# Two chained projections of a bidirectional layer, and one merged weight for each direction

## The chip, the cores and the metric

The kernel runs on one core of a Trainium2 chip. A core has a matrix engine (PE, with its weight loads shown apart as PEld), a vector engine (DVE), an activation engine (ACT), a general engine (POOL) and a queue for transfers (SP). Each engine works through its own instructions in the order in which the program issued them, and they wait for each other by semaphores. The metric is the device time of one execution in microseconds (us). The kernel before took 2102.75 us, the median of three runs (2097.81 to 2104.69).

## The reference

Four layers follow each other on a tensor of 2 batches, 1024 positions and 256 channels, all in 32-bit floats: a state-space layer (layer 0), a bidirectional state-space layer (layer 1), and two attention layers (2 and 3). What matters here is layer 1, cut to its projections:

```
mz  = x_ssm @ Wz.T + bz            # 256 -> 512 channels
mx  = x_ssm @ Wx.T + bx            # 256 -> 512
z1  = _ssm(mz @ Wc1.T + bc1, ...)  # 512 -> 512, then the forward scan
z2  = flip(_ssm(flip(mz @ Wc2.T + bc2), ...))   # 512 -> 512, then the backward scan
out = (silu(mx) * z1 + silu(mx) * z2) @ Wf.T + bf + skip
```

`mz` feeds nothing but the two projections `Wc1` and `Wc2`, and no nonlinearity stands between them. So `mz @ Wc1.T` equals `x_ssm @ (Wc1 Wz).T`, with a bias `Wc1 bz + bc1`.

A scan `_ssm` has 512 channels with 16 states each, over 1024 positions. Layer 0 has one scan for each batch, layer 1 two for each batch: six scans in all, s00, s01, s10, s20, s11, s21 (the first digit is 0 for layer 0, 1 and 2 for the two directions of layer 1; the second is the batch).

## The kernel before

**The scans set the order.** `chain` (line 1007) runs the six scans one after the other, each as 64 tiles of 128 rows (32 channels by 4 states) by 1024 positions, taken in pairs. A tile is one decay on ACT (`dA_t`, line 133 with `negA`), one product on POOL (`hb_t`, L952), one scan on DVE (L959 or L963), a second product on DVE (L966) or, for the first tile of some pairs, on POOL (L965), and a sum over states on PE (`fold`, L990), which is issued one pair later. Which engine takes the second product is decided by a running balance (`lead`) of the work that the program counted for DVE and POOL. The decay of the next tile is issued before the current one; there are two buffers of it, so it waits until DVE has finished the tile before the current one.

**Everything else is fitted in between.** The projections and norms of the layers are Python generators in one queue, worked off by `Behind`. Ahead of each tile stands one slot (`Behind.slot`, line 853): it adds a number of credits (`RATES`, line 32: 2048 in the first two scans, then 1250, 1300, 1500, 1500), holds the credit at 2048 at most, and runs steps while credit is above zero. A step costs the columns that its matmuls stream, or the number that it yields, and at least 640. Slots also have an allowance for ACT (2500 for each slot, up to 3400) and POOL (1500, up to 2300). Instructions of a step enter the engines' queues at that place, between those of the scan. Slots are counted here from 1 to 384: 1 to 64 belong to s00, 65 to 128 to s01, and so on.

The queue's order is p00 (layer 0, batch 0), two preparations of conditioning, p01 (layer 0, batch 1), p10 (layer 1, batch 0: norms, `mz`, `mx`, and the inputs of s10), p20 (the inputs of s20), a third preparation, p11 and p21 (the same for batch 1), then layers 2 and 3 of batch 0. p10 can only begin once the output projection of s00 (`residual`, line 802) has run; that is put at the head of the queue five slots after it is registered, which is slot 74. Layer 2 needs the output of s20 and is held until slot 266 and the steps after it. Batch 1 of layers 2 and 3 runs behind the attention that follows the scans.

**The projections.** `projected` (line 506) makes 512 output channels as 4 blocks of 128 by 2 halves of 512 positions. One step issues one block and half: `project` (line 495) calls one matmul for each 128 input channels, so two for a 256-channel source (`mz`, `mx`) and four for a 512-channel source (the two directions). ACT takes the result from one of two PSUM banks (`bank`) and adds the bias; `pipe` (line 375) and `projected` both take a bank back before they fill it a third time. A 32-bit matmul call appears in the profile as two MATMUL instructions.

**The weights.** `weight` (line 348) loads them over the SP queue. Tiles of 128 by 1024 share four buffers; a load whose buffer is still read waits in the SP queue, and what is issued after it waits too. The same queue carries the scan inputs (`sp`, L913), saves (L120) and everything else.

Of the kernel before, what the change touches and what calls it, by code (L numbers as in the profile page):

```python
# [54 lines left out]
def kernel(ctx: ExitStack, tc: tile.TileContext, a: dict, out: bass.AP):  # L55
    nc = tc.nc
# [30 lines left out]
    def dbuf(shape, name):  # L87
        return dram.tile(list(shape), F32, tag=name, name=name)
# [92 lines left out]
    def col(name, i=0, n=1):  # L181
        at, size = _COLS[name]
        assert i + n <= size
        return cols[:, at + i : at + i + n]
# [101 lines left out]
    def cond_first():  # L286

        w = load_k("ada_w0", 2 * D)
        for _ in cond_cols(w, "ada_b0", 4, (2, 0, "ln_g0", "ln_b0", "aff0")):
            pass  # L290

        def gates():
            scb = spread_cond()
            brow, w = abuf((1, D)), abuf((P, 4, D))
            nc.sync.dma_start(brow, a["ada_row0"][:, 2 * D :])
            nc.sync.dma_start(
                w, a["ada_w0"][:, 2 * D :].rearrange("(k p) m -> p k m", p=P)
            )
            yield 3 * T
            cond["gate0"] = []  # L300
            yield from pipe(*(
                cond_rows(
                    [w[:, k, :] for k in range(4)], scb, brow, 0, b, f"gate0_{b}", cond["gate0"]
                )
                for b in range(B)
            ))

        return gates()
# [39 lines left out]
    def weight(name, k, width, at=0, k0=0, slots=0, tag=None):  # L348

        t = wp.tile(  # L350
            [P, k, width], F32, tag=tag or f"w{k * width}", name=f"w_{name}",
            bufs=4 if tag is None and k * width == 1024 else 1,
        )
        src = a[name].rearrange("(k p) m -> p k m", p=P)[:, k0 : k0 + k, at : at + width]
        if slots:
            save(slots, t, src)
        else:
            nc.sync.dma_start(t, src)
        return t
# [373 lines left out]
        )  # L733


    def layer1(b, st1, st2):

        mz = []
        xn = []

        def way(i):
            return [weight(f"c{i}_w", 2, DI, 0, k) for k in (0, 2)]

        def one_way(i, st, wz):
            w_xp, w_dt = weight(f"xp_w{i}", 4, R + 2 * N, slots=2), weight64(f"dt_w{i}", 2)
            st["u"] = dbuf((DI, T), f"u{i}{b}")
            z = []
            yield from projected(
                wz, mz, AF.Identity, lambda m: col(f"bc{i}", m), z, True, st["u"]
            )  # L750
            yield from ssm_inputs(f"{i}{b}", z, w_xp, w_dt, f"dt_b{i}", st)

        def first():
            xt = yield from halves_of(x_of[1][b])
            w_z, w_x = [[weight("xz_w", 2, DI, at)] for at in (DI, 0)]
            st1["x"] = dbuf((T, D), f"x1{b}")
            skip = []
            yield from normed(xt, skip)
            for v in skip:
                nc.vector.tensor_tensor(v, v, twice(cond["s1"][b], 4), ALU.mult)  # L760
                far_op(v, v, twice(cond["o1"][b], 4), ALU.add)
                yield
            o = []
            yield from normed(skip, o)
            for i, v in enumerate(skip):
                far_op(v, v, twice(cond["gate1"][b], 4), ALU.mult)
                yield
                far_op(xt[i], xt[i], v, ALU.add)
                save(3, positions(st1["x"], i), xt[i])
                yield  # L770
            xn.extend(abuf() for _ in range(2))
            yield from channels(
                o, xn, AF.Identity, lambda c: col("n2g", c), lambda c: col("n2b", c)
            )
            yield from projected(
                w_z, xn, AF.Identity, lambda m: col("bz", m), mz
            )
            wz1 = way(1)
            st2["g"] = dbuf((DI, T), f"g1{b}")
            yield from projected(  # L780
                w_x, xn, AF.Silu, lambda m: col("bx", m), [], False, st2["g"], st2["gates"]
            )
            wz2.append(way(2))
            yield from one_way(1, st1, wz1)

        def second():
            yield from one_way(2, st2, wz2[0])

        wz2 = []
        return first(), second()  # L790

    def load_src(src, bias, halves=(0, 1)):
# [740 lines left out]
    with ExitStack() as s:  # L1533
# [13 lines left out]
        p10, p20 = layer1(0, s10.st, s20.st)  # L1547
# [64 lines left out]
        for _ in range(7):  # L1612
            behind.step()
        behind.add(
            cond_first(), cond_later(), p01, p10, p20, cond_last(), p11, p21,
            layer2(0, x2[0], x3[0]), layer3(0, sts[0]),
        )
        chain(
# [23 lines left out]
def _layout(i):  # L1642
# [21 lines left out]
    def heads(v, const_at=None):  # L1664
# [45 lines left out]
        "emb_w2": f["L2_cond_film_emb_W"], "emb_w3": f["L3_cond_emb_w"],  # L1710
        "in_w": f["L0_cond_in_proj_w"].T, "xp_w0": f["L0_cond_x_proj_w"].T,
        "dt_w0": f["L0_cond_dt_proj_w"].T, "out_w0": f["L0_cond_out_proj_w"].T,
        "xz_w": np.concatenate([f["L1_cond_Wx"].T, f["L1_cond_Wz"].T], axis=1),
        "c1_w": f["L1_cond_Wc1"].T, "c2_w": f["L1_cond_Wc2"].T,
        "xp_w1": f["L1_cond_Wdbc1"].T, "dt_w1": f["L1_cond_Wdt1"].T,
        "xp_w2": f["L1_cond_Wdbc2"].T, "dt_w2": f["L1_cond_Wdt2"].T,
# [25 lines left out]
```

## Time and profile before

The profile is one execution. Its own total was not recorded apart from its span, which is 2094.2 us from the first to the last instruction; the median of the runs is 2102.75 us, 8.6 us more, for start and end and for the difference between executions.

| what | us |
|---|---|
| span | 2094.2 |
| scans, from the first scan instruction to the last | 64.5 to 1452.8 |
| attention and what runs behind it, after the last scan | 1459 to 2094 |
| DVE busy, whole span | 1748.3 |
| POOL busy, whole span | 1365.8 |
| PE busy, whole span | 1592.7 |
| ACT busy, whole span | 1140.8 |
| matmuls that read w_xz (mz and mx, both batches), busy | 65.7 |
| matmuls that read w_c1 and w_c2, busy | 129.5 |

How to read it: busy times are shares of an engine's own time, not of the path. Busy time of PE is modelled and overlaps, so that for dense stretches the time from one group's start to the next is the better price. An arrow in a waiting row points to the instruction that ended the wait. "SPq" and the like are an engine's issuing side.

### The profile page before, as it was taken

How to read it: one execution, taken by the hardware profiler on the slowest of the kernel's cores; microseconds unless marked ns; L12 is line 12 of the kernel's file. 1: busy time of each engine (PE TensorE's matmuls, PEld its weight loads, DVE VectorE, ACT ScalarE, POOL GpSimd, SP SyncE). 2: the span in 40 equal slices, each digit the busy share in tenths (PEclk: the TensorE clock that was granted, in tenths of full speed). 3: DMA queues.
4: the chain of work that ended last, by engine and by line, in shares of the span. 5: the costliest groups of instructions: out<-in, count | busy, mean ns of one | idle time of the engine just before them, and what ended most of it. 6: DMA issues, size and time to landing. Idle time of an engine off the chain costs nothing. (4 is left out here: it accounts for less than half of the span.)

```text
span 2094.2 us, 22957 instructions
## 1 busy us (share of the span) xinstructions
PE 1592.7 (76%) x8112; PEld 605.6 (29%) x8112; DVE 1748.3 (83%) x1742; ACT 1140.8 (54%) x1592; POOL 1365.8 (65%) x666
## 2 busy tenths in 40 slices
PE   7576876389685637887955657834999999999997
PEld 3132213033141302222311333201544333333333
DVE  5798898898998999998998999998767657777763
ACT  4665775476546345664555455532154556656665
POOL 0799997998999999899998979997102111000000
PEclk9698988599797558988976978966899999999999
DMA  3673367264853555556763345343200111010001
GB/s 120 253 251 103 130 238 263 69 207 144 289 182 115 188 169 187 179 171 210 251 213 111 103 160 165 122 133 99 82 1 1 39 25 18 24 51 1 1 1 38
DMA packets 112503, 267.55 MB, mean 128 GB/s; under 512 B 16154, under 2 KB 40603, under 8 KB 112388
## 3 DMA queue, kind: packets, MB, share of 16 engines
q1 hardware_dynamic: 112388, 266.09, 38.2%
q8 instruction: 64, 1.05, 0.2%
q14 instruction: 51, 0.42, 0.1%
HBM read 195.91 MB, written 67.90 MB: 126 GB/s over the span
## 5 line engine op out<-in xcount | busy, mean ns | idle before, releaser
L952 POOL TENSOR_TENSOR hb_t<-sp,bc 128x1024 f32<-128x1024 f32 x383 | 918.7, 2436 | 62.9 <-PE ys_t L990 28.7
L133 ACT ACTIVATE dA_t<-sp,negA 128x1024 f32<-128x1024 f32 x384 | 428.3, 1117 | 530.4 <-DVE hb_t L966 446.4
L963 DVE TENSOR_TENSOR_SCAN dA_t<-dA_t,hb_t 128x1024 f32<-128x1024 f32 x195 | 445.8, 2286 | 43.8 <-ACT dA_t L133 29.0
L1442 DVE TENSOR_REDUCE mh<-sc_t 128x1 f32<-128x512 f32 x512 | 327.4, 684 | 114.2 <-PE sc_t L1433 110.6
L990 PE MATMUL ys_t<-hb_t,fold 128*32 128x512 f32 x1536 | 278.7, 735 | 167.2 <-POOL hb_t L965 110.5
L133 ACT ACTIVATE hb_t<-sc_t 128x512 f32<-128x512 f32 x512 | 276.7, 595 | 190.8 <-PE sc_t L1433 190.6
L966 DVE TENSOR_TENSOR hb_t<-dA_t,bc 128x1024 f32<-128x1024 f32 x285 | 349.0, 1224 | 22.1 <-DVE dA_t L959 0.5
L1433 PE MATMUL sc_t<-act_t 32*128 32x512 f32 x2048 | 337.3, 651 | 10.6 <-DVE mh L1442 8.8
L965 POOL TENSOR_TENSOR hb_t<-hb_t,bc 128x1024 f32<-128x1024 f32 x99 | 236.3, 2387 | 16.3 <-DVE hb_t L963 15.6
L799 POOL TENSOR_TENSOR act_t<-act_t,row 128x1024 f32<-128x1024 f32 x8 | 19.1, 2397 | 340.1 <-PE sc_t L99 191.9
L959 DVE TENSOR_TENSOR_SCAN dA_t<-dA_t,hb_t 128x1024 f32<-128x1024 f32 x90 | 205.7, 2285 | 11.8 <-POOL hb_t L952 7.4
L1473 PE MATMUL av_t<-hb_t,act_t 128*32 128x256 f32 x2048 | 164.7, 393 | 1.3 <-DVE act_t L1481 1.3
L95 PE MATMUL bank_t<-act_t,w_c_w 128*128 128x512 f32 x256 | 129.5, 656 | 37.0 <-ACT act_t L133 37.0
L133 ACT ACTIVATE act_t<-bank_t,cols 128x512 f32<-128x512 f32 (+1 forms) x206 | 129.6, 675 | 37.6 <-PE bank_t L95 29.5
L1433 PEld LDWEIGHTS sc_t<-act_t 32*128 32x128 f32 x2048 | 110.7, 186 | 121.4 <-issue 78.3
L990 PEld LDWEIGHTS ys_t<-hb_t,fold 128*32 128x32 f32 x1536 | 39.0, 119 | 362.7 <-POOL hb_t L965 149.5
L963 DVE TENSOR_TENSOR_SCAN hb_t<-dA_t,hb_t 128x1024 f32<-128x1024 f32 x61 | 139.0, 2278 | 4.3 <-ACT dA_t L133 3.9
L141 POOL TENSOR_TENSOR act_t<-act_t 128x1024 f32<-128x1024 f32 x50 | 119.2, 2384 | 0.2
L95 PE MATMUL bank_t<-act_t,w_dt_w 64*128 64x512 f32 x96 | 71.2, 876 | 43.9 <-ACT act_t L133 38.5
L99 PE MATMUL bank_t<-ident,act_t 128*128 128x128 f32 x128 | 34.3, 422 | 91.4 <-ACT act_t L133 91.2
L1473 PEld LDWEIGHTS av_t<-hb_t,act_t 128*32 128x32 f32 x2048 | 42.3, 108 | 191.5 <-issue 178.6
L1378 POOL MEMSET act_t<- 128x1024 f32 x8 | 7.6, 951 | 130.4 <-PE sc_t L1433 130.4
(178 smaller groups left out, 1811.6 us busy)
## 6 DMA issues: line engine op xcount, KB each, us to landing
sp<-dt SPq DMA_DIRECT2D x192, 512.0 KB, 5.5
bc<-bc SPq DMA_DIRECT2D x48, 512.0 KB, 6.8
dt<-act_t SPq DMA_DIRECT2D x48, 512.0 KB, 5.7
u<-act_t SPq DMA_DIRECT2D x24, 512.0 KB, 3.0
fu<-u SPq DMA_DIRECT2D x96, 128.0 KB, 3.4
y<-y SPq DMA_DIRECT2D x96, 128.0 KB, 3.6
g<-act_t SPq DMA_DIRECT2D x16, 512.0 KB, 5.4
fg<-g SPq DMA_DIRECT2D x64, 128.0 KB, 3.2
```

Source lines behind the costliest of these rows:

```text
L95: nc.tensor.matmul(o, w, x, **kw)
L133: nc.scalar.activation(o, x, func, **kw)
L141: nc.gpsimd.tensor_tensor(o, x, y, op)
L952: engine.tensor_tensor(e, self.sp[c, 1], self.bc[0][k], ALU.mult)
L959: nc.vector.tensor_tensor_scan(h[:, ::-1], dA[:, ::-1], e[:, ::-1], 0.0, ALU.mult, ALU.add)
L963: nc.vector.tensor_tensor_scan(h, dA, e, 0.0, ALU.mult, ALU.add)
L965: return lambda: nc.gpsimd.tensor_tensor(e, h, self.bc[1][k], ALU.mult)
L966: nc.vector.tensor_tensor(e, h, self.bc[1][k], ALU.mult)
L990: nc.tensor.matmul(self.ys[d, cp][at : at + DS, :], fold, e[:, ts(ch, 512)], start=False, stop=(k == NK - 1),)
L1433: nc.tensor.matmul(ps, w[r, ts(at, P)], x[r, ts(wide_at, 512)], start=True, stop=True)
L1442: nc.vector.tensor_reduce(mh[n][:, t, ch, j : j + 1], ps, AX.X, ALU.max)
L1473: nc.tensor.matmul(sums.av[32 * j : 32 * j + 32, ts(part, 256)], sts[b]["v"][t // 2][:, t % 2, 4 * g + j, :], es[j // 2][:, at : at + 256] ...
```

## The change

The two chained projections of each direction become one. A new generator `merge` stands in the queue between p01 and p10. For each direction it loads the two halves of the direction's weight, forms `Wc Wz` with matmuls into PSUM (two blocks, four calls of 512 columns each), copies each block with ACT to a tile that stays for the whole program (`way1`, `way2`), forms `Wc bz` with sixteen calls of one column each, and adds the bias with one DVE instruction. p10, p20, p11 and p21 then project from the 256-channel `xn` with these tiles, so each step of a direction issues two calls instead of four, and the eight steps of `mz` with their ACT instructions are gone in p10 and p11. The weights are loaded once instead of once for each batch; `Wz` is loaded untransposed, `Wx` alone. The two resident tiles take 8 KB of each partition; the area set aside for descriptors of software transfers goes from its default to 1024 bytes, and every transfer in the profile is issued by the SP queue.

```diff
+    ways = {}
+
+    def merge():
+
+        w_z = weight("z_w", 4, D)
+        for i in (1, 2):
+            w_c = [weight(f"c{i}_w", 2, DI, 0, k) for k in (0, 2)]
+            w = const.tile([P, 2, DI], F32, tag=f"way{i}", name=f"way{i}")
+            o = const.tile([P, 4], F32, tag=f"wayb{i}", name=f"wayb{i}")
+            yield 3 * T
+
+            def both(c):
+                ps = bank()
+                for k in range(4):
+                    mm(
+                        ps, w_z[:, k, ts(c, P)], w_c[k // 2][:, k % 2, :],
+                        start=(k == 0), stop=(k == 3),
+                    )
+                return ps
+
+            def shift():
+                ps = bank()
+                for m in range(4):
+                    for k in range(4):
+                        mm(
+                            ps[:, m : m + 1], w_c[k // 2][:, k % 2, ts(m, P)], col("bz", k),
+                            start=(k == 0), stop=(k == 3),
+                        )
+                return ps
+
+            yield from pipe(
+                *((lambda c=c: both(c), lambda ps, c=c: act_copy(w[:, c, :], ps))
+                  for c in range(2)),
+                (shift, lambda ps: nc.vector.tensor_tensor(
+                    o, ps[:, :4], col(f"bc{i}", 0, 4), ALU.add
+                )),
+            )
+            ways[i] = w, o
+
     def layer1(b, st1, st2):
 
-        mz = []
         xn = []
 
-        def way(i):
-            return [weight(f"c{i}_w", 2, DI, 0, k) for k in (0, 2)]
-
-        def one_way(i, st, wz):
+        def one_way(i, st):
             w_xp, w_dt = weight(f"xp_w{i}", 4, R + 2 * N, slots=2), weight64(f"dt_w{i}", 2)
             st["u"] = dbuf((DI, T), f"u{i}{b}")
+            w, o = ways[i]
             z = []
             yield from projected(
-                wz, mz, AF.Identity, lambda m: col(f"bc{i}", m), z, True, st["u"]
+                [w], xn, AF.Identity, lambda m: o[:, m : m + 1], z, True, st["u"]
             )
...
-            w_z, w_x = [[weight("xz_w", 2, DI, at)] for at in (DI, 0)]
+            w_x = [weight("x_w", 2, DI)]
...
-            yield from projected(
-                w_z, xn, AF.Identity, lambda m: col("bz", m), mz
-            )
-            wz1 = way(1)
...
-            wz2.append(way(2))
-            yield from one_way(1, st1, wz1)
+            yield from one_way(1, st1)
 
         def second():
-            yield from one_way(2, st2, wz2[0])
-
-        wz2 = []
+            yield from one_way(2, st2)
+            xn.clear()
+
         return first(), second()
...
-            cond_first(), cond_later(), p01, p10, p20, cond_last(), p11, p21,
+            cond_first(), cond_later(), p01, merge(), p10, p20, cond_last(), p11, p21,
...
-    nc = bacc.Bacc("TRN2", target_bir_lowering=False, num_devices=1)
+    nc = bacc.Bacc(
+        "TRN2", target_bir_lowering=False, num_devices=1, dynamic_dma_scratch_size=1024
+    )
```

More of the change, by code (lines that the diff above doesn't have):

```diff
@@ L1712, in _layout @@
         "dt_w0": f["L0_cond_dt_proj_w"].T, "out_w0": f["L0_cond_out_proj_w"].T,
-        "xz_w": np.concatenate([f["L1_cond_Wx"].T, f["L1_cond_Wz"].T], axis=1),
+        "x_w": f["L1_cond_Wx"].T, "z_w": f["L1_cond_Wz"],
         "c1_w": f["L1_cond_Wc1"].T, "c2_w": f["L1_cond_Wc2"].T,
```

## The prediction

> **What bounds the kernel now.** I read the page first: its head, the engines' shares and the slices.
>
> ```profile
> span 2094.2 us, 22957 instructions
> PE 1592.7 (76%) x8112; PEld 605.6 (29%) x8112; DVE 1748.3 (83%) x1742; ACT 1140.8 (54%) x1592; POOL 1365.8 (65%) x666
> PE   7576876389685637887955657834999999999997
> DVE  5798898898998999998998999998767657777763
> POOL 0799997998999999899998979997102111000000
> ```
>
> Two programs follow each other. Up to slice 28 (1459 us) DVE and POOL are full and PE is not; after it PE is full. All that the change touches lies in the first part, so I read that part by stretches, in windows cut where a background generator begins or ends. The columns are PE, PEld, DVE, ACT and POOL busy, then clock and transfers.
>
> ```profile
> 334.70:363.00 28.30, 19.84 (x88) 12.75 (x88) 21.97 (x30) 5.92 (x6) 22.98 (x11) 0.86 0.67 225
> 416.50:439.00 22.50, 22.50 (x76) 7.71 (x75) 22.12 (x14) 14.46 (x18) 20.60 (x10) 0.95 0.60 192
> 464.20:492.90 28.70, 24.95 (x72) 9.16 (x71) 26.68 (x17) 16.26 (x18) 19.50 (x9) 0.94 0.64 213
> 547.40:598.10 50.70, 35.88 (x112) 12.59 (x111) 48.53 (x29) 22.65 (x26) 45.69 (x20) 0.83 0.83 292
> 796.40:826.10 29.70, 25.75 (x86) 8.34 (x85) 29.00 (x19) 16.03 (x20) 29.29 (x13) 0.92 0.52 175
> 859.30:906.00 46.70, 40.94 (x136) 13.99 (x135) 44.27 (x26) 24.65 (x27) 46.70 (x21) 0.96 0.59 179
> 963.70:1011.30 47.60, 37.01 (x113) 12.60 (x112) 46.21 (x28) 20.63 (x24) 46.14 (x21) 0.92 0.86 293
> 1359.20:1450.50 91.30, 35.01 (x156) 6.15 (x152) 87.24 (x52) 32.35 (x32) 90.87 (x40) 0.64 0.35 108
> ```
>
> Row 1 is the output projection of s00 (`residual`); rows 2 and 5 are `mz` of the two batches (7 and 9 slots); rows 3, 4, 6 and 7 the direction projections (9, 15, 14, 14 slots); row 8 is the end of the scans, where the background is empty (28 slots). The reader should divide: with nothing behind it a tile takes 91.3/28 = 3.26 us; with `mz` behind it 3.21 and 3.30; with a direction 3.19, 3.38, 3.34, 3.40. The work to be removed hardly stretches the scans. It fills PE (22.50 of 22.50 us in row 2), and PE isn't what the tiles wait for.
>
> Then the waits and the timeline, for what a late PE does.
>
> ```profile
> ACT dA_t L133 <- DVE hb_t L966: 446.4, 208, 13.2
> POOL hb_t L952 <- PE ys_t L990: 28.7, 18, 4.0
> DVE act_t L806 <- PE bank_t L95: 8.5, 4, 5.0
> ```
>
> ACT waits 446 us for DVE: each decay needs a buffer that DVE frees with the tile before. POOL waited 28.7 us for sums on PE. The third row is the important one: a background addition on DVE that reads PE's result holds DVE, with the scans queued behind it, once for 5.0 us. Last, the prices of PE, from the timeline.
>
> ```profile
> 483.90 7.13 PE L95 MATMUL bank_t<-act_t,w_c_w 128*128 128x512 f32 x16
> 12.18 5.71 PE L95 MATMUL bank_t<-sc,act_t 128*128 128x2 f32 x26 [0.64 <-DMA act_t<-in_ada_w]
> 701.71 3.58 PE L95 MATMUL bank_t<-sc,act_t 128*128 128x2 f32 x16
> ```
>
> Sixteen instructions are eight 512-column calls, so a step of four calls is 3.56 us and one of two calls 1.78. Two-column matmuls with a full weight each cost 0.22 us for each instruction (5.71/26, 3.58/16).
>
> **The change part by part.** Total work first. PE loses 16 `mz` steps and half of 32 direction steps, 48 x 1.78 = 85 us, and gains four blocks, 4 x 3.56 = 14, and two `shift` groups of 16 calls (32 instructions), 2 x 7.1 = 14. ACT loses 16 takes and gains 4 copies, some 12 x 0.68 = 8 us, beside 446 us of waiting for DVE. Seven 512 KB weight loads remain of twelve. DVE and POOL, which are full, lose nothing: no scan, product or norm goes. So the 57 us that PE saves net are worth only the stalls they caused.
>
> *What the removed work gives back.* From the rows above, DVE's idle time in the six stretches is 0.4 + 2.0 + 2.2 + 0.7 + 2.4 + 1.4 = 9 us, POOL's 1.9 + 9.2 + 5.0 + 0.4 + 0 + 1.5 = 18 us. Over the free pace of 3.26 the four directions and `mz` lie 15 x 0.12 + 14 x 0.08 + 14 x 0.14 and 9 x 0.04, together 5 us. I take 6 (the pace, and a little for the tiles after them), with ends of 0 and 18. Removing the rest of PE's work there shows next what is late already: DVE and POOL themselves.
>
> *Where merge lands.* I work the slots by the planner's rules. p01 gives its last step in slot 72. Slot 73, an empty wait before, takes merge's first step (three loads, cost 3072 from a credit of 2048). Slots 74 to 77 hold the four `residual` blocks and 78 their additions, as before. Merge goes on: a block in 79, a block in 80, and with 1792 credits in slot 81 all three of its next steps at 640: copy and `shift`, copy, addition. 82 has the second pair of loads, 83 and 84 blocks, 85 copy and `shift`, 86 the addition. p10, which began in 78, begins in 86.
>
> *The first addition.* DVE's last residual addition is at 354.7 in the trace. The norm statistics behind it (355.3 to 359.6) move back with p10, so the tiles of 78, 79 and 80 take 3 x 3.5 us (2.29 scan and 1.22 product) and DVE reaches slot 81 at 365.9. The copy that frees the bank for `shift` stands on ACT behind a decay that needs that same end, then 1.1 us decay and 0.7 copy: `shift` starts at 367.7 and ends 7.1 us later, at 374.8. The addition, and every scan behind it, waits 9 us. POOL is at most three or four products ahead and then stops too.
>
> *The second.* Slots 81 to 85 from 375 at 3.3 us bring DVE to slot 86 at 391.5. The copy in 85 comes behind DVE's end of slot 84's tile (388.2) plus 1.8, `shift` with a sum of the scan before it (1.1) ends at 398: 6.5 us. Together 15.5, with the two small additions 16 us. Ends: 0, if PE gets to `shift` ahead of DVE, and 28, all of merge's PE time bare; I take 16 because the row of L806 shows the same wait at 5.0 us for a shorter group (3.7 us) of matmuls.
>
> [...] The trace's loads for these matmuls are 186 to 338 ns. [...]
>
> *The loads.* One of the second direction's loads has no free buffer of the four until `shift` has read the first (374.8), and holds SP. Behind it stand scan inputs for the next group of eight slots, some 15 us away; loads of these weights land in 6.1 to 7.0 us, so I count 0, ends 0 and 10. The data are there at 381, before the block of slot 83 must end.
>
> *What moves.* Steps cost 18,944 credits fewer in p10 and 18,176 more in merge, so the inputs of s10 come within two slots of before. p20, p11 and p21 end 7, 21 and 33 slots earlier; but layer 2 is pinned to the output of s20 at slot 266, so the background's end (1359, 91 us before the scans' end) comes only some 7 slots sooner, and nothing waits for it. The attention starts when the scans end and keeps its 635 us.
>
> Sum: +16 - 6 = +10 us on the profiled execution, span 2094.2 to 2104. The median of 2102.75 stands 8.6 us (0.4%) above that span; I carry the difference over: 2113 us.
>
> **The rivals.** *Absorbed:* merge's wait lands just ahead of p10's norms, a stretch where DVE idled 8.9 us of 53.5 (44.63 busy from 363.0 to 416.5), partly waiting for POOL's additions. If POOL is then ahead, half of the 16 comes back, the gain takes the rest: +2, 2105. Against it: those additions are issued after the wait, so POOL can't do them during it.
>
> *Faster:* the one mechanism is PE saturation. If POOL's 18 us are all on the path, and `shift` is done before DVE needs it (0 instead of 16), the time is 2103 - 13 to -18, say 2088. For it: in row 3 POOL idles 9.2 of 28.7 us with PE nearly full. Against it: that stretch still runs at 3.19 us a tile. It decides from a merge wait below the gain of 6.
>
> *The SP queue:* the blocked load delays scan inputs by its whole wait, 10 us in addition: 2123. For it: SP's loads of scan inputs already wait 607 us for POOL's buffers over the scans, so SP runs close. Against: 15 us of lead.
>
> *No effect:* everything moved was hidden, merge too: within 6 us of before. Little speaks for it but that three of four L806 waits were short.
>
> **How the numbers follow.** Merge's wait outweighs the gain (2107 to 2124, likeliest 2113): 0.54. Absorbed or no effect (2097 to 2109): 0.21. Faster (2084 to 2096): 0.18. SP queue on top (2118 to 2130): 0.07. The range 2092 to 2126 leaves out half of the faster case and the far ends of the slower ones. A measurement can tell about 0.3%, 6.3 us: faster 0.18, same 0.21, slower 0.61.
>
> **What the profile after would show.** Right: DVE idle at two `wayb` additions near 366 and 391, 9 and 6.5 us, ended by PE; tiles under the directions still 3.2 to 3.4 us apart, POOL's waits for sums smaller; an empty background from about slot 248 to 266; scans ending some 10 us later; 635 us of attention unchanged. Wrong: additions that hardly wait, or tiles that come at 3.1 us where PE was full. The prediction fails if the balance between DVE and POOL, both at the limit, shifts by the new order of the background, which no row of before can show.

## The result and the profile after

The changed kernel takes 2110.47 us (median of 12 runs, 2107.28 to 2117.99) against 2103.0 us for the kernel before on the same chip (12 runs, 2091.09 to 2107.44). The ratio is 1.0043 with a 95% interval of 1.0028 to 1.0059: slower by 9 us by the ratio (6 to 12 us), 7.5 us between the two medians. Forecast were +10 us on the profiled execution and, with the same step, a median of 2113 us. The profiled execution of the changed kernel took 2108.51 us, 2 us below its median.

The head of the page of the changed kernel, with the shares:

```profile
span 2106.8 us, 22753 instructions
PE 1571.7 (75%) x8016; PEld 598.8 (28%) x8016; DVE 1751.0 (83%) x1744; ACT 1134.7 (54%) x1580; POOL 1357.3 (64%) x666
```

PE is busy 21 us less and the span is 12.6 us longer. By the groups of matmuls the change takes 62 us net off PE, but the scans' sums over states, the same 1536 matmuls, take 305.5 us instead of 278.7, at a mean granted clock of 0.827 instead of 0.851. VectorE (DVE) has the same work (1751.0 against 1748.3 us). What became longer is the time in which it stands. Measured from the first tile of the second scan to the last tile, the stretch is 1148.5 us before (DVE busy 1069.4, idle 79.2) and 1156.0 after (1069.7 and 86.2).

The timeline of the changed kernel around the merge; each line gives start and length, and in brackets the idle time before and what ended it:

```profile
367.02 6.99 PE L95 MATMUL bank_t<-cols,w_c_w 128*128 128x1 f32 x32 [2.50 <-ACT way L137]
374.04 0.16 DVE L769 TENSOR_TENSOR wayb<-bank_t,cols 128x4 f32<-128x4 f32 x1 [8.74 <-PE bank_t L95]
376.49 2.35 POOL L996 TENSOR_TENSOR hb_t<-hb_t,bc 128x1024 f32<-128x1024 f32 x1 [7.51 <-DVE hb_t L994]
388.51 4.83 PE L95 MATMUL bank_t<-cols,w_c_w 128*128 128x1 f32 x32 [2.87 <-ACT way L137]
393.37 0.16 DVE L769 TENSOR_TENSOR wayb<-bank_t,cols 128x4 f32<-128x4 f32 x1 [3.81 <-PE bank_t L95]
```

Here is the wait that the prediction put in the place of the removed work. An addition of 0.16 us stands 8.74 us for 32 small matmuls, the scans stand behind it, and POOL stops 7.51 us too, because it has run out of buffers that DVE frees. The second addition stands 3.81 us.

Groups of waits of the changed kernel between 60 and 1470 us (engine and line, what it waited for, total, times, longest):

```profile
POOL hb_t L983 <- PE ys_t L1021: 30.6, 19, 4.9
DVE wayb L769 <- PE bank_t L95: 12.6, 2, 8.7
DVE rq L1275 <- ACT t L133: 5.2, 3, 1.7
DVE qmx L1259 <- PE bank_t L95: 3.4, 2, 3.1
```

The last two rows had not been forecast. They belong to layer 2, which moved some seven slots sooner, and come back below. The slots that carry the four direction projections, and in the last row the end of the scans (columns as in the windows before: PE, PEld, DVE, ACT, POOL busy, clock, transfers):

```profile
478.19:504.11 25.92, 22.00 (x66) 8.02 (x66) 22.31 (x14) 17.64 (x22) 20.66 (x10) 0.93 0.63 195
538.49:570.65 32.16, 21.81 (x63) 6.75 (x62) 31.46 (x21) 18.57 (x22) 32.16 (x15) 0.89 0.77 266
808.96:840.63 31.67, 26.02 (x84) 8.19 (x77) 29.08 (x17) 20.46 (x25) 31.10 (x14) 0.89 0.70 223
887.71:922.61 34.90, 27.60 (x75) 8.75 (x76) 34.24 (x23) 18.78 (x23) 34.90 (x16) 0.85 0.69 231
1367.40:1460.50 93.10, 36.14 (x156) 6.50 (x152) 89.58 (x53) 33.40 (x32) 92.50 (x41) 0.66 0.33 106
```

In the first four rows DVE is idle 3.6, 0.7, 2.6 and 0.7 us, 7.6 together, in 35 slots. By the same measure (from the scan that runs when the first direction matmul starts to the first scan that starts after the last one has) the kernel before has 18.5 us in 59 slots. So per slot the idle time fell from 0.31 to 0.22 us; a good part of the 11 us between the sums is only that fewer slots carry these calls. One stall of the kernel before is missing from the prediction's third window, which ends at 492.90 us, just ahead of it:

```profile
500.93 2.30 DVE L963 TENSOR_TENSOR_SCAN dA_t<-dA_t,hb_t 128x1024 f32<-128x1024 f32 x1 [4.43 <-ACT dA_t L133]
```

The last row above shows DVE and POOL alone at the limit, as before the change (93.10/29 = 3.21 us a tile, 3.26 before).

How far the tiles of the changed kernel and of the experiments are behind the kernel before, at some tiles of the six scans (counted from 0; one profiled execution each, in us):

| kernel | 1/0 | 1/16 | 1/32 | 2/0 | 4/0 | 4/32 | 4/48 | 5/8 | last tile |
|---|---|---|---|---|---|---|---|---|---|
| changed | 2.6 | 4.2 | 10.1 | 9.2 | 8.6 | 2.4 | 13.8 | 10.1 | 10.0 |
| no merge | 0.5 | 6.2 | 3.8 | -0.5 | -1.0 | 0.7 | 3.0 | 7.8 | 4.6 |
| late additions | 0.1 | -5.2 | -1.7 | -2.7 | -3.1 | -7.8 | 4.6 | 1.1 | 1.8 |
| offset twice | 2.8 | 11.4 | 24.2 | 23.3 | 25.8 | 20.4 | 30.9 | 27.5 | 28.1 |
| split | -1.3 | -6.8 | -2.4 | 10.5 | 4.2 | 9.4 | 22.7 | 17.4 | 14.0 |
| late, two empty steps | 0.6 | -5.4 | -1.9 | -3.1 | -2.9 | 1.4 | 4.2 | 15.0 | 13.1 |
| calls made twice | 0.2 | 3.9 | 1.6 | 17.5 | 22.8 | 24.4 | 26.7 | 36.2 | 32.8 |

Two things limit what such a row can tell. The 2.6 us at tile 1/0 of the changed kernel come from a scan whose instructions are the same, so that much is noise. And a profiled execution lies up to 15 us from its kernel's median. In the runs that have both, the time stands 1.7 us above the span; by that the profiled execution of the kernel before took an estimated 2095.9 us, 7 below its median, and every row is measured against this early one. So totals are taken below from the ratios (one hundredth of a per cent is 0.21 us) and only places and mechanisms from the profiles.

### The profile page after: what moved, and what is told of

Same layout as the page of the kernel before. It is cut to its first block, busy times and chain, and to the rows that moved or that the text cites. A ratio compares the mean times of both kernels' runs of the same rounds, so it can differ in the third digit from the quotient of the medians.

```text
span 2106.8 us, 22753 instructions
## 1 busy us (share of the span) xinstructions
PE 1571.7 (75%) x8016; PEld 598.8 (28%) x8016; DVE 1751.0 (83%) x1744; ACT 1134.7 (54%) x1580; POOL 1357.3 (64%) x666
## 5 line engine op out<-in xcount | busy, mean ns | idle before, releaser
L983 POOL TENSOR_TENSOR hb_t<-sp,bc 128x1024 f32<-128x1024 f32 x383 | 909.6, 2403 | 61.4 <-PE ys_t L1021 30.6
L1021 PE MATMUL ys_t<-hb_t,fold 128*32 128x512 f32 x1536 | 305.5, 784 | 207.1 <-POOL hb_t L996 136.9
L1464 PE MATMUL sc_t<-act_t 32*128 32x512 f32 x2048 | 336.7, 653 | 12.4 <-DVE mh L1473 8.9
L994 DVE TENSOR_TENSOR_SCAN hb_t<-dA_t,hb_t 128x1024 f32<-128x1024 f32 x65 | 148.0, 2277 | 8.3 <-ACT dA_t L133 8.0
L133 ACT ACTIVATE act_t<-bank_t,cols 128x512 f32<-128x512 f32 (+1 forms) x158 | 97.9, 678 | 32.6 <-PE bank_t L95 32.5
L95 PE MATMUL bank_t<-act_t,way 128*128 128x512 f32 x128 | 69.6, 684 | 25.0 <-ACT act_t L133 25.0
```

The lines of the kernel that those rows point to most:

```text
L95: nc.tensor.matmul(o, w, x, **kw)
L133: nc.scalar.activation(o, x, func, **kw)
L983: engine.tensor_tensor(e, self.sp[c, 1], self.bc[0][k], ALU.mult)
L994: nc.vector.tensor_tensor_scan(h, dA, e, 0.0, ALU.mult, ALU.add)
L1021: nc.tensor.matmul(self.ys[d, cp][at : at + DS, :], fold, e[:, ts(ch, 512)], start=False, stop=(k == NK - 1),)
L1464: nc.tensor.matmul(ps, w[r, ts(at, P)], x[r, ts(wide_at, 512)], start=True, stop=True)
```

## The experiments

### The removed work without the merge

```diff
-        w_z = weight("z_w", 4, D)
...
-            w_c = [weight(f"c{i}_w", 2, DI, 0, k) for k in (0, 2)]
...
-            yield from pipe(
...
+            nc.sync.dma_start(
+                w, a[f"c{i}_w"].rearrange("(k p) m -> p k m", p=P)[:, 0:2, :]
             )
-            ways[i] = w, o
+            ways[i] = w, col(f"bc{i}", 0, 4)
```

> Left out: the merge's computation; the two resident weights are simply loaded (half of Wc1 and Wc2), so the output is another one. What stays is the removed work alone: no mz, half of the direction calls, p10 in its old place. My theory (the change gives back about 6 us of stalls, and merge costs 12.6 us by two DVE additions that wait for PE): 6 us below before, 2097. Rival (the background's new order costs the time, and merge's waits are absorbed): 2103 or more. Rival (PE was the hidden limit under the projections): 2090 or less.

Measured: 2100.78 us, ratio 0.9986 (0.997 to 1.0002), that is -3 us, with -6 to 0 in the interval. That lies between the theory's -6 and the first rival's 0; the second rival, PE as a hidden limit, is out. In the slots that carry the direction projections DVE is idle 4.8 us in 32 slots, where the kernel before has 18.5 in 59. Over the whole stretch from the second scan on it falls only from 79.2 to 77.6. Part of the rest came back elsewhere: the waits of the residual additions for PE are 14.8 us in seven here, 8.5 in four before. So the work taken off PE freed the places where it was late, and other blocks, which now fall into other slots, were late instead. The removed work was worth some 3 us as this kernel stands. A further 7 us of it may be hidden by one instruction of layer 2, told below.

### The merge without the offset

The offset of a way is the bias of the first projection carried through the second: the 16 one-column calls and the addition. Without them the old bias `col(f"bc{i}", 0, 4)` is used.

```diff
             yield from pipe(
                 *((lambda c=c: both(c), lambda ps, c=c: act_copy(w[:, c, :], ps))
                   for c in range(2)),
-                (shift, lambda ps: nc.vector.tensor_tensor(
-                    o, ps[:, :4], col(f"bc{i}", 0, 4), ALU.add
-                )),
             )
-            ways[i] = w, o
+            ways[i] = w, col(f"bc{i}", 0, 4)
```

> Left out: the bias part Wc bz (the sixteen one-column calls and the addition for each direction), so the output lacks it; every step falls in the same slot but the addition's. My theory: 12 us below the changed kernel, 2098. Rival (the blocks of merge and the move of p10 by eight slots cost the time): 2108 or more.

Measured: 2100.65 us, ratio 1.001 (0.9989 to 1.003), 6.9 us below the changed kernel by the ratios where the theory had 12; the rival (2108 us or more) is out. What is left of the change, the merged products and the seven or eight slots by which they move p10 (its first norm instruction comes at tile 84, in the kernel without a merge at tile 77), leaves the kernel at +2, 5 us above the kernel without a merge. That these 5 us are there is not shown: the two intervals overlap, and the two medians agree within 0.2 us. They come from three of the twelve executions, which took 2114 to 2115 us where the other nine took 2096 to 2104. The profiled one is of the three: it loses 10.9 us after tile 5/8, and in it PE is busy 25 of 25 us at clock 0.50 from 1280 to 1305 us.

### The same additions, three slots later

```diff
-                (shift, lambda ps: nc.vector.tensor_tensor(
+                (shift, lambda ps, i=i, o=o: later(3, lambda: nc.vector.tensor_tensor(
                     o, ps[:, :4], col(f"bc{i}", 0, 4), ALU.add
-                )),
+                ))),
```

> Everything computed; each of the two additions is issued three slots later, and no other step changes its slot. My theory: the waits of 8.7 and 3.8 us are gone, 11 to 12 us below the changed kernel, 2099. Rival (the burst of one-column matmuls on PE delays the sums of the scans, whoever reads it): POOL's wait for sums grows and the time stays at 2107 or more. Rival (the wait was absorbed by the idle time under p10's norms): within 3 us of the changed kernel.

Measured: 2105.42 us, ratio 1.0013 (0.9997 to 1.0029), 6.3 us below the changed kernel. PE does every one of the merge's calls, in the same slots; only the order on DVE differs. The timeline of this kernel:

```profile
366.49 5.28 PE L95 MATMUL bank_t<-cols,w_c_w 128*128 128x1 f32 x32 [2.50 <-ACT way L137]
373.87 0.15 DVE L769 TENSOR_TENSOR wayb<-bank_t,cols 128x4 f32<-128x4 f32 x1
383.43 5.17 PE L95 MATMUL bank_t<-cols,w_c_w 128*128 128x1 f32 x32
399.65 0.15 DVE L769 TENSOR_TENSOR wayb<-bank_t,cols 128x4 f32<-128x4 f32 x1
```

Neither addition has a bracket: neither waits. At tile 1/32 this execution is 11.8 us ahead of the changed kernel's (-1.7 against 10.1), about the 12.6 us of waiting. POOL's waits for sums are 29.1 us, 30.6 in the changed kernel, so the rival that the burst of small matmuls delays the scans' sums, whoever reads it, is out. This and the run above agree that the two additions' waits cost 6 to 7 us at the end, some 2 to 12 us by the intervals. That is most of the 9 us; of the other 2.7 it is not shown that they are there.

### The offset's calls twice

```diff
-                for m in range(4):
+                for m in (0, 1, 2, 3, 0, 1, 2, 3):
```

> The changed kernel with each one-column call of the offset product made twice into the same columns: 32 calls (64 matmuls of one column) instead of 16 for each way, no step in another slot. Theory (the VectorE addition behind these calls is a wait that reaches the end): the calls took 7.0 and 4.8 us, so each addition comes about 7 and 5 us later; the waits read about 15.7 and 8.7 us instead of 8.7 and 3.8, and the end comes 11 to 12 us after the changed kernel's, about 2121 us. Rival (the wait is mostly made up for by the backlog later on): up to 5 us. Below 2 us, the additions are not what the change costs.

Measured: 2130.69 us, ratio 1.0145 (1.0111 to 1.0178), 21 us above the changed kernel. The timeline:

```profile
368.87 12.28 PE L95 MATMUL bank_t<-cols,w_c_w 128*128 128x1 f32 x64 [2.50 <-ACT way L137]
381.18 0.16 DVE L769 TENSOR_TENSOR wayb<-bank_t,cols 128x4 f32<-128x4 f32 x1 [14.04 <-PE bank_t L95]
395.65 11.79 PE L95 MATMUL bank_t<-cols,w_c_w 128*128 128x1 f32 x64 [2.94 <-ACT way L137]
407.47 0.16 DVE L769 TENSOR_TENSOR wayb<-bank_t,cols 128x4 f32<-128x4 f32 x1 [10.77 <-PE bank_t L95]
```

The waits read 14.0 and 10.8 us where 15.7 and 8.7 were expected; the sum, 24.8, is as expected (24.4). The time is not: 12.3 us of added waiting cost 21 (14 to 29 by the intervals). In the table the kernel is 14.1 us behind the changed one at tile 1/32 and 18.1 at the last, and nothing in between makes it good. Three of its six executions read 2125 to 2126 us, 15 above the changed kernel, and three 2135 to 2145; what the latter add has no profile. A wait that is absorbed is out; that its price is above its length is seen and not explained.

### The second way's merge later

The second way's products were moved behind the next part's steps, and each addition comes after two empty steps.

```diff
-        for i in (1, 2):
+        if True:
...
+            ps = shift()
+            held[0] += 1
+            yield
+            for _ in range(2):
+                yield 2 * T
+            nc.vector.tensor_tensor(o, ps[:, :4], col(f"bc{i}", 0, 4), ALU.add)
+            held[0] -= 1
+            yield
...
-            cond_first(), cond_later(), p01, merge(), p10, p20, cond_last(), p11, p21,
+            cond_first(), cond_later(), p01, merge(1), p10, merge(2), p20, cond_last(), p11, p21,
```

> Everything computed; only the first direction's merge stands before p10, the second's stands between p10 and p20, each addition comes after two empty steps. p10 begins some slots earlier than in the changed kernel. My theory: waits gone as with the later addition, 2099. Rival (moving p10's norms away from the residual is what costs): better than the later addition by 3 us or more, 2095; if merge's blocks stall the scans wherever they stand: 2103.

Measured: 2119.36 us, ratio 1.008 (1.0058 to 1.0103), 17 us above the kernel before. The timeline shows another wait in the place of those removed:

```profile
550.96 8.69 PE L95 MATMUL bank_t<-w_c_w,w_z_w 128*128 128x512 f32 x16 [22.35 <-DMA w_c_w<-in_c_w]
556.26 0.58 ACT L137 COPY way<-bank_t 128x512 f32<-128x512 f32 x1 [12.17 <-PE bank_t L95]
561.40 2.30 DVE L999 TENSOR_TENSOR_SCAN dA_t<-dA_t,hb_t 128x1024 f32<-128x1024 f32 x1 [11.49 <-ACT dA_t L133]
```

So the merge in that place was held up by its loads. PE stands 22.35 us for the weights, which were asked for only two slots ahead; ScalarE (ACT) stands 12.17 us at its copy of the bank, the decay stands behind the copy, and DVE behind the decay, 11.5 us. In the table the kernel goes from -2.4 to +10.5 between tiles 1/32 and 2/0.

### The same with early loads

```diff
+        if i == 1:
+            parts["z"] = weight("z_w", 4, D)
+            parts[1] = [weight("c1_w", 2, DI, 0, k) for k in (0, 2)]
...
+            if i == 1:
+                w_c = None
+                parts[2] = [weight("c2_w", 2, DI, 0, k) for k in (0, 2)]
```

> The kernel with the second way's merge moved behind the next part's steps, as in the split one, but its two weights loaded right after the first merge rather than two slots before their use. Nothing is left out. Theory (the split one lost its 17 us because the loads came late: TensorE stood 22 us for the weights, and through the copy VectorE 11.5 us): that wait goes, and the time falls to that of the late additions or below, 2098 to 2106 us. Rival (a block of merging matmuls costs about as much wherever it stands among the blocks of a scan): it stays above 2112 us.

Measured: 2108.65 us, ratio 1.003 (1.0008 to 1.0052). The blocks also come about five tiles sooner than in the split kernel (at tile 123 of the count from 0, there at 128), since the step ahead of them no longer costs the credits of a load; so the loads are not the only difference. 10.5 us of the 17 go, and no gap of DVE above 1.5 us is left between 500 and 620 us, where the split kernel had 11.5. So the wait for late loads was most of its loss, though the time lies between the theory's 2106 us and the rival's 2112. The kernel still is 6 us above the one before, although its DVE is idle only 72.3 us from the second scan on, 7 less than before (the profiled execution, 2101.34 us, is one of the six of twelve that took 2100 to 2107 us; the other six took 2110 to 2118). What takes the place is busy time, 1079.4 us against 1069.4, most of it one instruction, which the last point of this section shows.

### PE's load put back

To the kernel without a merge, each direction step's calls a second time into the same bank, with the slots kept. As in its parent the merged product is not formed.

```diff
+                ps = project(w, src, m, ch)
+                at = work[0]
+                for _ in range(times - 1):
+                    project(w, src, m, ch, ps)
+                work[0] = at
+                waiting.append((m, ch, ps))
```

> The kernel whose ways are simply loaded and not merged, with each of the two projections' calls made twice into the same bank, so that TensorE has back about as much work as the change took away (64 calls of 512 columns, some 70 us busy), with every step in the same slot. As in its parent the merged product is not formed, so the output is another. Theory A (what the removed work gives back is TensorE's lateness in its blocks): it takes back the 3 us, and comes to the level of the kernel before (ratio 1.000 to 1.004). Theory B (less work only lowers the granted clock, and the time of a block stays): no slower than its parent, ratio 0.997 to 1.000, with a mean clock above the parent's 0.815.

Measured: 2127.3 us, ratio 1.0129 (1.0105 to 1.0153), 30 us above its parent. Neither theory had that. The groups of waits of this kernel:

```profile
DVE dA_t L972 <- ACT dA_t L133: 42.6, 20, 8.9
```

23.1 us in 15 in its parent. PE's group in one slot takes 7.1 us, about twice a tile's time, so ACT's next step waits for PE with the decays behind it. In the first direction's slots DVE is idle 12.3 us (1.3 in the parent), in those of all four 25.8 (4.8), which is 21 of the 30 us. About the same amount of work that was worth 3 us when it went costs 30 us when it comes in two calls at the place of one. By these waits, what counted was whether a block's calls end before ACT's take of them comes up, and not PE's total.

### Layer 2's steps in other slots, and the clock

In the kernel before, layer 2's step with the exponentials and its step that reduces their sums on DVE fall into different slots; in the changed one into the same, and DVE waits (rows `rq` and `qmx` above). Two empty steps ahead of layer 2, on top of the late additions, part them again. (The steps do not meet in the kernel without a merge either, although layer 2 starts in it as early.)

```diff
+    def spare(n):
+
+        yield from halves_of(x_of[2][0])
+        for _ in range(n):
+            yield
...
-            layer2(0, x2[0], x3[0]), layer3(0, sts[0]),
+            spare(2), layer2(0, x2[0], x3[0]), layer3(0, sts[0]),
```

> The kernel with the additions issued three slots later, and two empty steps ahead of layer 2 of the first batch, so that in its loop over queries the step with the exponentials and the step with the row sums' reduction come in different slots again, as they do before the change. Nothing is left out. Theory (after the merge's wait the rest of the loss is this meeting in one slot): the waits of VectorE for ScalarE's exponentials there (5.2 us for three in the changed kernel) go, and it ends about 5 us earlier than with the late additions alone, some 2100 us, level with the kernel before. Rival (which slots these two steps fall in costs nothing that lasts): the same as with the late additions alone, some 2105 us.

Measured: 2113.71 us, ratio 1.0051 (1.0032 to 1.0069), 8 us slower than the late additions alone. The theory falls as far as the time goes. The `rq` waits are gone, and from tile 4/32 to 4/48 this kernel loses 2.8 us where late additions alone lose 12.4. But from 4/0 to 4/32 it loses 4.3 where its parent gains 4.7, and from 4/48 to 5/8 it loses 10.8 where its parent gains 3.5. In the last of these stretches the windows of this kernel show PE at half clock for 20 us:

```profile
1240.00:1260.00 20.00, 20.00 (x44) 10.06 (x44) 7.89 (x7) 6.85 (x7) 8.46 (x4) 0.50 0.58 205
1260.00:1270.00 10.00, 8.90 (x44) 3.25 (x36) 8.02 (x12) 1.12 (x1) 8.91 (x4) 0.88 0.42 158
```

PE is busy 20.00 of 20.00 us and DVE 7.89. A residual's group of four matmuls takes 2.08 us in the first row and 1.13 in the second. The next run takes the idle time ahead of it away with products of zero weights:

```diff
+        def fill(self, d, cp, n):
+
+            for _ in range(n):
+                for ch in range(2):
+                    for j in range(2):
+                        at = 64 * ch + DS * j
+                        nc.tensor.matmul(
+                            self.ys[d, cp][at : at + DS, :], none,
+                            ident.unsqueeze(1).to_broadcast([P, 4, P]),
+                            start=False, stop=False,
+                        )
...
+            n, at[0] = 3 if 152 <= p <= 157 else 0, work[0]
```

> The kernel with late additions and two empty steps, with six pairs of tiles at the end of the fifth scan given three more products of zero weights each (24 matmuls of 512 columns into the same accumulation, which add nothing), so that TensorE does not stand idle in the 35 us ahead of the residual's calls. In its parent the granted clock was 0.50 over nearly all of 1210 to 1262 us, the residual's groups of four took 2.08 us there and 1.13 us right after, and VectorE waited 19.4 us for their banks. Theory (TensorE's clock halves when it has little to do and comes back late, and this is what the empty steps ran into): the clock there reads 0.9 or more, the groups take about 1.1 us, most of the 19.4 us goes, and the time falls by 8 to 12 us, to about 2102 to 2106 us. Rival (so many calls in one stretch hold VectorE up at any clock): the clock rises but the time stays above 2110 us.

```profile
1240.00:1260.00 20.00, 18.59 (x101) 7.85 (x94) 10.34 (x8) 10.41 (x11) 14.14 (x6) 0.95 0.38 117
```

The clock is back and DVE's waits for the residual's banks fall from 19.4 to 9.7 us, as the theory said. The time does not follow: 2112.62 us, ratio 1.0053 (1.0036 to 1.0071). In the profiled executions the stretch from tile 4/48 to 5/8 is 6.6 us shorter, and both reach 5/8 at +15.0, since this one had lost 5.7 us by 4/0 with the same instructions. The half clock is real and local; it is not what these 8 us are.

### The same filling everywhere

Three such products behind each pair of tiles, fewer where the background gave PE calls, in the changed kernel, with the late additions, and in the kernel before:

```diff
+            n, at[0] = max(0, 3 - (work[0] - at[0]) // 512), work[0]
```

> The changed kernel with products of zero weights behind each pair of tiles of all six scans: three (24 matmuls of 512 columns) where the background gave TensorE nothing since the last pair, two, one or none where it gave one, two, or three and more calls of 512 columns. Nothing is left out. Theory (part of the change's loss is the halved clock after idle stretches: the first way's 32 one-column matmuls ran at 0.50): the mean clock rises above 0.95, the first addition's wait falls from 8.7 to 5 or 6 us, and the time falls by 5 to 15 us to 2095 to 2105 us. Rival (added work on TensorE delays its calls as in the kernel with the doubled calls): 2115 us or more.

Measured: 2114.14 us, ratio 1.007 (1.0055 to 1.0086).

> The same filling products in the kernel with the additions issued three slots later. Theory of the clock: 5 to 15 us below its parent's 2105 us, so about 2090 to 2100 us, below the kernel before and the changed one; rival (load): above 2110 us.

Measured: 2110.71 us, ratio 1.0043 (1.0029 to 1.0056).

> The same filling products in the kernel before the change. It has 85 us more of TensorE's own work and a clock of 0.851. If the halved clock costs every version about alike, it gains as much as the changed kernel with them, 5 to 15 us, and the change's loss of 7.5 us stays between the two. If the change itself had brought the low clock, it gains less, 0 to 5 us, and the two come together. Rival (load): it loses 5 us or more, since it has the least room on TensorE.

Measured: 2120.33 us, ratio 1.0092 (1.0077 to 1.0106).

The clock theory falls as far as the time goes: the mean clock rises from 0.827 to 0.896 in the changed kernel and from 0.851 to 0.903 in the one before, and all three become slower, as the rivals of load had it (the first of the three falls just short of its 2115 us). Its local part held: in the changed kernel the first way's 32 small matmuls take 4.83 us instead of 6.99, and the waits of the additions fall from 8.74 and 3.81 to 6.59 and 3.25 us. What these runs show best is PE's room. The groups of the changed kernel with filling, and then of the kernel before with it:

```profile
L1034 PE MATMUL ys_t<-ident,none 128*32 128x512 f32 x2192 | 307.1, 660 | 0.0
```

```profile
L1003 PE MATMUL ys_t<-ident,none 128*32 128x512 f32 x1784 | 251.7, 659 | 0.0
```

307 us of useless PE work cost the changed kernel 5.7 us; 252 us cost the kernel before 19. So the change did make room on PE, as its diff says, and with this load on both it is the changed kernel that is faster (2114 against 2120 us, though the ends of the two intervals touch). Without the load nobody needs that room.

### One instruction of layer 2

DVE's busy time from the second scan on lies between 1069 and 1081 us in the fourteen traces. Without one instruction, layer 2's mask (1024 integers to floats), it lies between 1067 and 1072. From the timeline of the changed kernel:

```profile
1086.81 2.38 POOL L983 TENSOR_TENSOR hb_t<-sp,bc 128x1024 f32<-128x1024 f32 x1
1088.59 1.15 DVE L1182 TENSOR_SCALAR act_t<-act_t 128x1024 f32<-128x1024 int32 x1
1091.02 2.39 POOL L983 TENSOR_TENSOR hb_t<-sp,bc 128x1024 f32<-128x1024 f32 x1 [1.84 <-PE ys_t L1021]
```

And from that of the kernel with late additions and two empty steps:

```profile
1076.06 4.78 POOL L983 TENSOR_TENSOR hb_t<-sp,bc 128x1024 f32<-128x1024 f32 x2
1076.92 11.45 DVE L1188 TENSOR_SCALAR act_t<-act_t 128x1024 f32<-128x1024 int32 x1
1080.80 2.37 POOL L996 TENSOR_TENSOR hb_t<-hb_t,bc 128x1024 f32<-128x1024 f32 x1
1083.11 4.71 POOL L983 TENSOR_TENSOR hb_t<-sp,bc 128x1024 f32<-128x1024 f32 x2
```

In eight kernels (before, changed, no offset, late additions, offset twice, the three with filling everywhere) it takes 1.15 to 1.25 us and POOL pauses after the product beside it. In the other six it takes longer: 7.3 (split), 8.2 (split with early loads), 8.3 (no merge), 8.3 (calls twice), 11.4 and 11.5 (the two with empty steps), and POOL has two to four more products ready. In all fourteen it ends 0.55 us after the last product of POOL's run. It ends only when POOL has no further product ready, and while it runs DVE frees nothing for POOL, so the length looks like POOL's lead; that is argued from these traces. What holds it is not shown: with two empty steps it takes 11.45 us, beside five of POOL's products in a row.

This is 10.2 us of extra DVE time in the kernel with empty steps, which lost 8 us to its parent; 7.1 us in the kernel without a merge; and 7.0 in the split one with early loads. Read so, the removed work would be worth some 10 us instead of 3, and the split merge with early loads would end level with the kernel before or a little below. These two sums are worked out and not measured: no kernel was run in which that instruction alone is moved. The changed kernel has the short form, as the one before, so this is no part of its loss. But it can stand in for another part of it. Of the changed kernel and the eleven made from it, six have the short mask, and all six have 5.2 us of `rq` waits; the other six have the long mask, and all but the split one (6.9 us) have no `rq` wait. The kernel before, with filling and without, has neither. So the runs that take away the meeting in layer 2 bring the long mask in its place, and no run shows the change with neither.

## Why the prediction was right, and where it was not

- **What bounds the kernel.** Right, and stronger than told: DVE and POOL pace the scans, and PE takes 307 us more for 5.7 us. The reading that a tile takes 3.19 to 3.40 us with a direction behind it rests on windows that leave out the ends of these stretches; by whole slots it is 3.35 to 3.72. PE's removed work was sized well: the direction and `mz` matmuls lost 59.9 and 29.2 us of busy time, 89 together (85 forecast); the blocks of the merge take 15.0 (14) and the one-column groups 11.8 (14). The net saving, 57 us forecast and 62 by these groups, shows as only 21 us of PE's busy time.
- **Where the merge lands.** Right slot for slot: 73 and 79 to 86. The first addition was reached at 365.3 us (365.9 forecast) and released at 374.0 (374.8).
- **The first addition.** 8.7 us for 9 forecast; the mechanism was as told, with POOL stopping behind it.
- **The second addition.** 3.8 us for 6.5. The mis-sized term is the length of `shift`: 7.1 us was taken for both from rows of two-column matmuls, of which the one at 701.71 us ran at clock 0.50, and the second took 4.83 us. The granted clock was 0.50 from 370 to 375 us, under the first one; it was 1.00 from 380 to 390 and 0.59 from 390 to 395, across the second (388.5 to 393.3). The shortest such group seen, the second in the split kernel and in the one with two empty steps, took 3.73 us.
- **Their price.** The term of 16 us, taken as all on the path, was too large: 12.6 us of waiting are worth 6 to 7 us, by two experiments that take the waits away in different ways (2 to 12 us by the intervals). The absorbed rival, which gave back half, describes this term well; but twice the calls cost 21 us more, so the half is no rule.
- **What the removed work gives back.** 6 us forecast, 3 measured (0 to 6), between its ends of 0 and 18. Without the merge, DVE's idle time in the slots with direction matmuls fell by 14 us (18.5 in 59 slots, 4.8 in 32), and over all the scans by 1.6: the failure is that it came back at other places.
- **The merge's own blocks and copies** were counted at nothing beside DVE, and so was the later start of p10. By the ratios they leave about 5 us between the kernel without a merge and the one without the offset; by the medians nothing. If the 5 us are there, the sum of +10 came close to the +9 because an overpriced wait stood against this term and against a gain that was taken as twice its size. So it was right in direction by its main step, and in amount partly by luck.
- **The loads.** Right: a load of the second way held SP from 357.93 for 15.62 us, and DVE's wait for scan inputs is 9.0 us (8.9 before). The SP rival is out for the changed kernel. Loads that come late have the price that was feared, though: with the split merge they cost most of the 17 us.
- **What moves.** "Nothing waits for it" failed for layer 2. It starts some seven slots sooner, as forecast, but its steps now fall on each other differently: 8.6 us of waits on DVE (5.2 and 3.4; 0 and 0.5 before), and 11.4 us lost between tiles 4/32 and 4/48. Since tiles just before had gained, and the run that parted the steps was slower, by its trace through the mask, what this costs in the end stays open.
- **What the profile would show.** The scans end 10.0 us later, as told; the stretch from the last tile to the end is 646.3 us (643.7). The background is empty from tile 245 to 265 of the count from 0, as told, and ends at tile 349 instead of 355. POOL's waits for sums did not become smaller (30.6 us, 28.7 before). The direction slots run at 3.49 to 3.70 us a tile by the slots that carry calls, not at 3.2 to 3.4; before the change they read 3.35 to 3.72 by that measure, so the pace hardly depended on these calls.
- **The faster rival** needed an addition that doesn't wait. With late additions it does not wait, and the kernel still ends at 1.0013, so it was further off than its condition said: even without a merge the ratio is 0.9986, and its interval ends at 0.997.

## What to carry to other kernels

Work removed from an engine that was not the bound was worth less here than the stalls read from the stretches where it ran: DVE's idle time fell by 14 us in those slots, by 1.6 over the scans, and the time by 3. Ask instead what the new work makes the bounding engine wait for. A tiny instruction with the scans queued behind it can cost many times its length: the two additions of 0.16 us waited 12.6 us, and issuing them three slots later took away all of that waiting and 6.3 us of the time. Where many generators share slots, moving one changes which steps meet (the 5.2 us of `rq` waits), so a change should be compared with a kernel that keeps the slots. And for a lone instruction like the mask, 1.15 to 1.25 us where POOL paused and 7.3 to 11.5 where it had products ready, a place where POOL is idle anyway is worth a trial; no run shows it there.

## What the runs showed of the hardware

- One VectorE instruction of 1.2 us took 7.3 to 11.5 us beside back-to-back GpSimd products, and always ended 0.55 us after the last of them (fourteen traces). VectorE's products (1.22 us) kept their length beside GpSimd's (2.4 us): in the kernel before, 228 of 285 overlap one for more than half of their time, and the mean is 1.224 us with or without.
- With less work TensorE's granted clock was lower: 0.84 to 0.85 in the executions before, 0.815 to 0.827 in those of the changed kernel, 0.815 to 0.831 without the merge. In the trace before, 71 stretches of 5 us have PE busy 2 us or less; the next 5 us read 0.55 or lower in 56 of them. How soon full clock comes back differs: PE was busy all the time at 0.50 for 5 to 10 us in most places, for 20 us in the kernel with two empty steps (1240 to 1260) and for 25 in the one without the offset (1280 to 1305) and in the one with the calls made twice (1255 to 1280). At 0.50 the same group of four matmuls takes 2.08 us instead of 1.13.
- More clock did not buy time here. Where products of zero weights raised it from 0.50 to 0.95 (1240 to 1260 us), VectorE's waits for PE's banks were halved (19.4 to 9.7 us), and the kernel's time stayed within 1 us by the ratios.
